# Attention scores of two units in ten full steps instead of sixteen of four widths, in a post-norm transformer block on one core

## The chip, the cores and the metric

The kernel runs on one core of a Trainium2 chip. The metric is the device time of one execution in microseconds (us); lower is better. TensorE is called PE here, VectorE DVE, ScalarE ACT, GpSimd POOL, and SyncE SP, as in the profile.

## The reference

The input x is 8 batches of 512 tokens of 256 features. Everything is float32. The block computes attention with a memory term, a layer norm, a mixture of eight experts, and a second layer norm. Cut to what matters:

```python
qkv = (x @ qkv_w.T + qkv_b).reshape(B, T, 3, H, dh)          # B 8, T 512, H 16 heads, dh 16
scores = einsum('bhtd,bhsd->bhts', q, k) * dh ** -0.5
scores = where(causal, -inf, scores)
seq_out = einsum('bhts,bhsd->bhtd', softmax(scores), v)
# four more projections of x give "write" and "read" lines of each head; decayed sums over the
# tokens of their outer products, read by the read lines, give one gate per token:
gated = mean over heads of sigmoid(mem_score * mem_scale) * sigmoid(x @ memg_w.T + memg_b)
x = layernorm(x + (seq_out + gated * (x @ memv_w.T + memv_b)) @ out_w.T + out_b)
# experts: softmax over ten gates, the two largest, eight true experts of 256 x 256
combine_w = weights of the two chosen experts, normed over the true ones
x = layernorm(x + einsum('te,teh->th', combine_w, einsum('td,edh->teh', x, expert_w) + expert_b))
```

## The kernel before

**Units.** The attention of a batch is done in four units of four heads (`UNITS`, 32 in all). `project_qk` makes, for two units at a time, q and k with the four heads of a unit on four strips of 32 partitions. A score product thus has a contraction of 32 rows, and products of different strips can stand beside each other on TensorE.

**Two kinds of products.** Softmax needs the largest score of each query. So each score is computed twice. The first time, `mx` (L194), has queries on the partitions and keys along the columns; DVE reduces it to the negated row maximum (`negmax`, `negdia`). `turn_largest` transposes the maxima of a unit and a DMA (`qk<-nt`) puts them into a spare row of q. The second time, `sc` (L198), has keys on the partitions and queries along the columns, with the maximum already subtracted by that spare row; ACT takes the exponential into `pe` (L226), POOL clears what is not causal on the diagonal block (L228), and `values` (L250) multiplies `pe` with v into one bank `po`, which also gets the sums for the division.

**Causal widths.** With four tiles of 128 tokens, query tile t has 128 (t + 1) keys that count, and key tile j has 512 - 128 j queries. So there are products of 128, 256, 384 and 512 columns.

**Steps.** One call of `products(u, i, pr)` is a step: the maxima of unit u + 1 for one query tile and two heads, on two strips, and beside them the scores of unit u (or u - 1) for one key tile of the same width and two heads, on the other two strips. A unit has eight steps, two for each width. `mx` and `sc` have one buffer each of two banks, one bank for each head (`psA`, bufs=1).

**The mask of the maxima.** For the first 12 units (`BYPASS`), and for a unit's last step later, a product of a bfloat16 mask with the identity (L207, 128 columns) adds -1e30 to the diagonal block, and DVE reduces the whole at once (L208). Otherwise ACT copies the diagonal block out (`dia`, L212), POOL masks the copy (L213), DVE reduces the rest of the row (L216), and one step later the copy (L219).

**What fills the time between steps.** Everything else is written as generators: the lines and the memory sums (`lines`, `memory_sums`, `finish`), the preparation of a batch (`prepare`), its attention output and first norm (`front`: `pa`, `px`, `pg`), and its experts (`all_experts`: `pex` L772 with two DVE operations L776 each, `pbias`). After each step, `fill` adds a credit, the step's share in `TAKE` less what is fixed there (projections `PQ`, `PV`, values `PO`), plus `MORE` (or `EARLY` before the first batch is ready), and lets the generators go on until their stated costs have used it up. What of the share finds no work is filled with idle products (`warm`, L843). A generator that yields `STEP`, `POOL`, `LESS` or `CALM` goes on only at a later turn, or only when POOL has not been given too much in this one. The order on each engine is then exactly the order in which the program was written (`in_this_order`).

**Buffers.** `psB` has three banks for all other products; `pe` has four buffers; `po` one bank. SP's queue issues nearly all DMAs.

Of the kernel before, what the change touches and what calls it, by code (L numbers as in the profile page):

```python
# [20 lines left out]
NG = 4  # L21
# [5 lines left out]
TAKE = (0.85, 1.6, 1.35, 1.1)  # L27
EARLY, MORE = 0.6, 0.9
WARM = 0.3
PV, PQ, PO = 1.2, 2.15, (1.05, 0.85, 0.65, 0.45)  # L30
ROUNDS = (2, 1, 1, 1)
# [14 lines left out]
for _n, _w in (("ob", D), ("gb", NE), ("mgb", H), ("msc", H), ("dec", H), ("mix", 1)):  # L46
    ROW[_n] = (_at, _at + _w)
    _at += _w
# [29 lines left out]
def block_kernel(ctx, tc, x, xT, wqk, bqk, wtok, wod, memv, memvb, row, gw, we, eb, out):  # L78
# [26 lines left out]
    nc.gpsimd.dma_start(rows, row.to_broadcast([P, NROW]))  # L105
# [17 lines left out]
    for b in range(1, B):  # L123
# [10 lines left out]
    mask_ts = const.tile([P, P], BF16, name="mask_ts")  # L134
    nc.gpsimd.memset(mask_ts, 0.0)
    nc.gpsimd.affine_select(out=mask_ts, in_=mask_ts, compare_op=ALU.is_ge, fill=MASKED,
                            base=0, pattern=[[-1, P]], channel_multiplier=1)
# [16 lines left out]
    ob2 = const.tile([P, D], F32, name="ob2")  # L154
# [3 lines left out]
    UNITS = [(b, g) for b in range(B) for g in range(NG)]  # L158
    qk = {}
# [24 lines left out]
    def products(u, i, pr):  # L184
        m, t = u + 1, (0, 3, 2, 1)[i]
        v, j = (u, i - 1) if i else (u - 1, NT - 1)
        n = T - j * P
        mx = m < len(UNITS) and psA.tile([P, 2, T], F32, tag="mx", name=f"mx{m}_{t}_{pr}")
        sc = 0 <= v < len(UNITS) and psA.tile([P, 2, T], F32, tag="sc", name=f"sc{v}_{j}_{1 - pr}")
        for h in range(2):  # L190
            if mx:

                r = slice(32 * (2 * pr + h), 32 * (2 * pr + h) + 32)
                nc.tensor.matmul(mx[:, h, :n], qk[m, 0][r, n - P : n], qk[m, 1][r, :n], start=True, stop=m >= BYPASS and (i, pr) != LAST)  # L194
            if sc:

                r = slice(32 * (2 - 2 * pr + h), 32 * (2 - 2 * pr + h) + 32)
                nc.tensor.matmul(sc[:, h, :n], qk[v, 1][r, j * P : (j + 1) * P], qk[v, 0][r, j * P :], start=True, stop=True)  # L198
        behind = list(diagonal)
        diagonal.clear()  # L200
        if mx:
            if m not in negmax:
                negmax[m] = [att.tile([P, 4, NT], F32, name=f"{n_}{m}", tag=n_) for n_ in ("negmax", "negdia")]
            most, least = (v[:, 2 * pr : 2 * pr + 2, t] for v in negmax[m])
            if m < BYPASS or (i, pr) == LAST:
                for h in range(2):
                    nc.tensor.matmul(mx[:, h, n - P : n], identb, mask_ts, start=False, stop=True)  # L207
                nc.vector.tensor_reduce(least, mx[:, :, :n], AX.X, ALU.max, negate=True)  # L208
            else:

                dia = ffp[0].tile([P, 2, P], F32, tag="dia", name=f"dia{m}_{t}_{pr}")
                nc.scalar.copy(dia, mx[:, :, n - P : n])  # L212
                nc.gpsimd.affine_select(out=dia, in_=dia, compare_op=ALU.is_ge, fill=MASKED,  # L213
                                        base=0, pattern=[[0, 2], [-1, P]], channel_multiplier=1)
                if t:
                    nc.vector.tensor_reduce(most, mx[:, :, : n - P], AX.X, ALU.max, negate=True)  # L216
                diagonal.append((least, dia))
        for to, dia in behind:
            nc.vector.tensor_reduce(to, dia, AX.X, ALU.max, negate=True)  # L219
        if mx and m >= BYPASS and (i, pr) == LAST:  # L220
            most, least = negmax[m]
            for hs, ts in ((slice(0, 2), slice(1, NT)), (slice(2, 4), slice(2, NT))):
                nc.vector.tensor_tensor(least[:, hs, ts], least[:, hs, ts], most[:, hs, ts], ALU.min)
        if sc:
            pe = att.tile([P, 2, T], F32, tag="pe", name=f"pe{v}_{j}_{1 - pr}", bufs=4)
            nc.scalar.activation(pe[:, :, :n], sc[:, :, :n], AF.Exp, scale=DH**-0.5)  # L226

            nc.gpsimd.affine_select(out=pe[:, :, :P], in_=pe[:, :, :P], compare_op=ALU.is_ge, fill=0.0,  # L228
                                    base=0, pattern=[[0, 2], [1, P]], channel_multiplier=-1)
            pes[j, 1 - pr] = pe  # L230

    def turn_largest(u):

        pt = bank(f"pt{u}")
        nc.tensor.transpose(pt[:H, :P], negmax.pop(u)[1].rearrange("p j i -> p (j i)"), ident)
# [4 lines left out]
    negmax, diagonal = {}, []  # L240
    LAST = NT - 1, 1
    pes, pos = {}, {}

    def values(u, j):

        b, g = UNITS[u]
        if j == 0:
            pos[u] = psO.tile([P, T], F32, tag="po", name=f"po{u}")
        for h in range(4):
            nc.tensor.matmul(pos[u][32 * h : 32 * h + 32, j * P :], v_aug[b % 2][:, j, 4 * (g // 2) + h, g % 2 : g % 2 + 2].rearrange("p q d -> p (q d)"),  # L250
                             pes.pop((j, h // 2))[:, h % 2, : T - j * P] if h % 2 else pes[j, h // 2][:, 0, : T - j * P],
                             start=(j == 0), stop=(j == NT - 1))
        if j == NT - 1:
# [10 lines left out]
    def invert(b, part):  # L264

        s = st[b]
        if part == 0:
            s["rec"] = att.tile([P, T // 8], F32, name=f"rec{b}", tag="rec")
            nc.sync.dma_start(s["rec"], s["den"].rearrange("k j q (e t) -> (k j q e) t", e=8))
# [18 lines left out]
    def fold_values():  # L288
# [9 lines left out]
        for n in range(2):  # L298
# [7 lines left out]
            else:  # L306
                nc.vector.tensor_tensor(ob2, pw[:, :D], vec("ob"), ALU.add)
# [161 lines left out]
    def memory_sums(half):  # L469
# [35 lines left out]
        for n, (h, c) in enumerate(todo):  # L505
# [24 lines left out]
            if rounds[1] >= ROUNDS[(turn[0] - 1) // 2 % NT]:  # L530
# [6 lines left out]
    def finish(half, h0, rm):  # L537
# [8 lines left out]
        for n, to, by in ((1, sm, of_heads), (2, sm2, rm)):  # L546
            for c in range(0, NT, 2):
                cs = slice(c, c + 2)
                yield LESS
                q = memp.tile([P, 2, 8 * HALF, 6], F32, tag="q", name=f"q{n}{half}_{h0}_{c}", bufs=2)  # L550
# [274 lines left out]
    def advance(it):  # L825
# [5 lines left out]
        elif asks == CALM and (at == turn[0] or turn[0] % (2 * NT) == 0):  # L831
            return None
        elif asks == STEP and at == turn[0] or asks == POOL and turn[1] or asks == LESS and turn[1] > 1:
# [11 lines left out]
    def fill(need, most=3.0, least=0.0):  # L845
# [5 lines left out]
    def filled():  # L851
        turn[:] = turn[0] + 1, 0
        for it in list(chains):
            for _ in range(2):
# [33 lines left out]
    U = len(UNITS)  # L888
    for u in range(-1, U + 1):
        b, g = UNITS[u] if 0 <= u < U else (0 if u < 0 else B, -1)  # L890
        for i in range(NT if u < U else 2):
            for pr in range(2):
                need = TAKE[i]
                if (i, pr) == (0, 0) and 0 <= u < BYPASS:
                    turn_largest(u)
                    need -= 0.3
                products(u, i, pr)
                if pr == 0:
                    if i == 0 and BYPASS <= u < U:
                        turn_largest(u)  # L900
                        need -= 0.3
                    if u % 2 == 0 and u + 2 < U and i in (1, 2):
                        project_qk(u + 2, i - 1)
                        need -= PQ
                    if g == NG - 1 and b + 1 < B:
# [81 lines left out]
```

## Time and profile before

| | us |
|---|---|
| median of 3 runs (lowest, highest) | 933.14 (932.42, 936.82) |
| span of the profiled execution, first to last instruction | 931.2 |
| PE busy, matmuls (5280) | 863.4 |
| PE busy with weight loads (overlap the matmuls) | 415.6 |
| DVE busy (1460) | 625.8 |
| ACT busy (754) | 346.5 |
| POOL busy (726) | 383.9 |
| first and last score group | 11.3 and 805.3 |

The profile gives no other time for its execution than the span; the median of the runs is 1.9 us above it, and that is taken for what lies around the first and the last instruction. A row of the costliest groups names the line, the engine, the operation, out<-in by the program's names, the shapes and the count, then the busy time and the mean of one in ns, then the idle time of the engine just before, with what ended it. PE's records overlap each other, since matmuls are pipelined and their ends are modelled; what a group costs is therefore read from its start to the start of what follows.

### The profile page before, as it was taken

Reading aid. Unit: us, or ns where it says so; the run is one execution under the profiler, and the core shown is the slowest. Engines: PE = TensorE matmul, PEld = TensorE weight load, DVE = VectorE, ACT = ScalarE, POOL = GpSimd, SP = SyncE. Lnnn points to the kernel's source line nnn. Section 1 sums busy time; section 2 is a strip of 40 time slices with the busy share of each in tenths; the row PEclk is TensorE's granted clock in tenths of the full one; section 3 lists DMA queues with packets and bytes.
Section 4 is the critical chain, followed back from the end, with each engine's and each line's share of the span. In section 5 each row is a group of like instructions: output and inputs, shape, how many; then the busy total and the mean of one; then the engine's idle time right before and its main releaser. Section 6 shows DMA issues by size and latency. Waiting matters only on the chain.

```text
span 931.2 us, 14645 instructions
## 1 busy us (share of the span) xinstructions
PE 863.4 (93%) x5280; PEld 415.6 (45%) x5280; DVE 625.8 (67%) x1460; ACT 346.5 (37%) x754; POOL 383.9 (41%) x726
## 2 busy tenths in 40 slices
PE   8999978788899889999999999999999999989997
PEld 5545444444355444453435344534353335344443
DVE  2344678986876787768685667666666675577765
ACT  4355624344334434435444444353434332100000
POOL 1168684526483855424353245324532352110000
PEclk9999989999999999999999999999999999989999
DMA  7300000000010101000200010001100010010000
GB/s 256 102 13 14 8 7 5 2 2 2 29 46 2 48 5 46 2 1 5 70 1 2 3 48 24 2 5 35 36 2 3 26 47 1 3 47 0 23 28 17
DMA packets 25512, 23.73 MB, mean 25 GB/s; under 512 B 8348, under 2 KB 21180, under 8 KB 25440
## 3 DMA queue, kind: packets, MB, share of 16 engines
q1 hardware_dynamic: 24336, 22.24, 7.5%
q8 instruction: 41, 0.67, 0.3%
q10 hardware_dynamic: 1056, 0.40, 0.2%
q0 software_dynamic: 48, 0.16, 0.2%
q14 instruction: 31, 0.25, 0.1%
HBM read 16.75 MB, written 4.73 MB: 23 GB/s over the span
## 4 chain that ended last, share of the span: by engine, by line
PE 63%; DVE 20%; POOL 6%; issue 4%; ACT 4%; DMA 3%; ACTq 0%; POOLq 0%; SPq 0%; DVEq 0%
PE pex L772 22%; PE mx L194 13%; PE po L250 6%; PE pq L167 4%; PE pa L653 3%; PE pa L656 3%; DVE negdia L208 3%; DVE x L776 3%; PE sc L198 2%; DVE negmax L216 2%; DMA s<-w 2%; PE pv L177 2%; DVE ou L520 2%; DVE pr L522 2%; DVE rm L502 1%
## 5 line engine op out<-in xcount | busy, mean ns | idle before, releaser
L194 PE MATMUL mx<-qk,qk 32*128 32x128 f32 (+3 forms) x1024 | 221.4, 486 | 35.9 <-DVE negdia L208 23.9
L772 PE MATMUL pex<-ws,x1T 128*128 128x512 f32 x512 | 243.7, 613 | 5.5 <-DVE x L776 4.9
L226 ACT ACTIVATE pe<-sc 128x1024 f32<-128x1024 f32 (+3 forms) x256 | 181.5, 709 | 144.6 <-PE sc L198 137.2
L198 PE MATMUL sc<-qk,qk 32*128 32x512 f32 (+3 forms) x1024 | 211.2, 485 | 3.0 <-DMA qk<-nt 1.8
L776 DVE SCALAR_TENSOR_TENSOR x<-pex,cw,x 128x256 f32<-128x256 f32 x256 | 123.2, 481 | 90.6 <-PE pex L772 85.3
L228 POOL TENSOR_SCALAR_AFFINE_SELECT pe<-pe 128x256 f32<-128x256 f32 x256 | 105.7, 413 | 176.1 <-ACT pe L226 170.2
L194 PEld LDWEIGHTS mx<-qk,qk 32*128 32x128 f32 x1024 | 85.4, 184 | 147.6 <-DVE negdia L208 41.4
L772 PEld LDWEIGHTS pex<-ws,x1T 128*128 128x128 f32 x512 | 92.0, 192 | 118.4 <-issue 101.2
L208 DVE TENSOR_REDUCE negdia<-mx 128x2 f32<-128x512 f32 (+3 forms) x116 | 92.3, 795 | 68.1 <-PE mx L207 67.4
L213 POOL TENSOR_SCALAR_AFFINE_SELECT dia<-dia 128x256 f32<-128x256 f32 x140 | 57.3, 409 | 178.7 <-ACT dia L212 178.5
L212 ACT COPY dia<-mx 128x256 f32<-128x256 f32 x140 | 52.1, 372 | 209.5 <-PE sc L198 203.9
L216 DVE TENSOR_REDUCE negmax<-mx 128x2 f32<-128x768 f32 (+2 forms) x100 | 74.0, 740 | 47.4 <-ACT dia L212 46.6
L250 PE MATMUL po<-pe,v_aug 128*32 128x512 f32 (+3 forms) x1024 | 96.7, 450 | 0.4 <-POOL pe L228 0.4
L198 PEld LDWEIGHTS sc<-qk,qk 32*128 32x128 f32 x1024 | 79.3, 184 | 11.9 <-issue 4.5
L167 PE MATMUL pq<-xt,wq 128*128 128x512 f32 x128 | 64.7, 630 | 3.3 <-DVE x L787 2.7
L219 DVE TENSOR_REDUCE negdia<-dia 128x2 f32<-128x256 f32 x140 | 57.4, 410 | 7.9 <-POOL dia L213 7.9
L171 ACT ACTIVATE qk<-pq,bq 128x512 f32<-128x512 f32 x64 | 46.2, 774 | 27.5 <-PE pq L167 27.5
L512 PE MATMUL pm<-ou,dm 128*128 128x144 f32 x256 | 46.6, 312 | 2.4 <-DVE pr L522 2.3
L631 POOL TENSOR_TENSOR rr_b<-rs_b,half 128x4 f32<-128x4 f32 (+1 forms) x11 | 9.2, 840 | 95.8 <-DVE rs_b L629 95.7
L512 PEld LDWEIGHTS pm<-ou,dm 128*128 128x128 f32 x256 | 36.9, 198 | 18.3 <-issue 13.5
L483 POOL TENSOR_TENSOR ou<-jw,jf 128x288 f32<-128x288 f32 x64 | 44.3, 698 | 1.3
L843 PE MATMUL idle<-ident 128*128 128x128 f32 x192 | 35.3, 313 | 2.9 <-POOL ident masks.py:199 2.8
(175 smaller groups left out, 1031.5 us busy)
## 6 DMA issues: line engine op xcount, KB each, us to landing
xt<-in_xT SPq DMA_DIRECT2D x8, 512.0 KB
x<-in_x SPq DMA_DIRECT2D x8, 512.0 KB
recs<-dr SPq DMA_DIRECT2D x16, 256.0 KB
out_y<-x SPq DMA_DIRECT2D x32, 128.0 KB
ws<-in_we SPq DMA_DIRECT2D x2, 1024.0 KB
s<-w SPq DMA_DIRECT2D x8, 127.0 KB
qk<-nt ACTq DMA_DIRECT2D x32, 8.0 KB
wq<-in_wqk SPq DMA_DIRECT2D x3, 128.0 KB
```

The source lines that it names most:

```text
L167: nc.tensor.matmul(pq, wq[:, k, w, g // 2, :], xt[:, b, k, :], start=(k == 0), stop=(k == KC - 1))
L194: nc.tensor.matmul(mx[:, h, :n], qk[m, 0][r, n - P : n], qk[m, 1][r, :n], start=True, stop=m >= BYPASS and (i, pr) != LAST)
L198: nc.tensor.matmul(sc[:, h, :n], qk[v, 1][r, j * P : (j + 1) * P], qk[v, 0][r, j * P :], start=True, stop=True)
L208: nc.vector.tensor_reduce(least, mx[:, :, :n], AX.X, ALU.max, negate=True)
L216: nc.vector.tensor_reduce(most, mx[:, :, : n - P], AX.X, ALU.max, negate=True)
L219: nc.vector.tensor_reduce(to, dia, AX.X, ALU.max, negate=True)
L226: nc.scalar.activation(pe[:, :, :n], sc[:, :, :n], AF.Exp, scale=DH**-0.5)
L228: nc.gpsimd.affine_select(out=pe[:, :, :P], in_=pe[:, :, :P], compare_op=ALU.is_ge, fill=0.0, base=0, pattern=[[0, 2], [1, P]], channel_mu ...
L250: nc.tensor.matmul(pos[u][32 * h : 32 * h + 32, j * P :], v_aug[b % 2][:, j, 4 * (g // 2) + h, g % 2 : g % 2 + 2].rearrange("p q d -> p (q ...
L512: nc.tensor.matmul(pm[:, i * HALF * 36 : (i + 1) * HALF * 36], dms[h + i], ou[:, i], start=True, stop=True)
L772: nc.tensor.matmul(pe, x1T[:, k, c * P : (c + 1) * P], ws[:, k, 2 * ep : 2 * ep + 2, :].rearrange("p e h -> p (e h)"), start=(k == 0), sto ...
L776: nc.vector.scalar_tensor_tensor(x1[:, c, :], pe[:, e * D : (e + 1) * D], cw[:, c, 2 * ep + e : 2 * ep + e + 1], x1[:, c, :], ALU.mult, AL ...
```

## The change

The scores of two units (a pair) are cut into ten steps that each fill the two banks of `mx` and of `sc`, 512 columns for each head. A step holds one piece of 512, or two pieces of 128 and 384, or two of 256 that belong to the two units of the pair. `mx` runs seven steps ahead of `sc` (`LAG`). A mask product now covers the whole bank (512 columns, L227 of the kernel after) and comes first in its step, with `start=True`; the row products add to it. The masks are needed in all ten steps of the first six pairs and in two steps (`LASTS`) of the others. The value products of earlier steps stand between the masks and the row products, one or two key tiles at a time, so that five steps of ten have them. The diagonal copies of a step with two pieces hold 512 columns in place of 256. The exponential always covers 1024 columns. The shares of `fill` are set anew: `TAKE` 1.9 for every step, `MORE` 1.5 and `EARLY` 1.0, at most two memory products a step, POOL's limits a step raised. To make room, three small tiles are smaller: the bias of the output is loaded straight into `ob2` by its own DMA, `rec` has one buffer, and `q` in `finish` holds one query tile in place of two.

The diff, cut to its core:

```diff
-TAKE = (0.85, 1.6, 1.35, 1.1)
-EARLY, MORE = 0.6, 0.9
+TAKE = 1.9
+EARLY, MORE = 1.0, 1.5
-ROUNDS = (2, 1, 1, 1)
+ROUNDS = 2
...
-    nc.gpsimd.dma_start(rows, row.to_broadcast([P, NROW]))
+    nc.gpsimd.dma_start(rows, row[:, D:].to_broadcast([P, NROW]))
+    ob2 = const.tile([P, D], F32, name="ob2")
+    nc.gpsimd.dma_start(ob2, row[:, :D].to_broadcast([P, D]))
...
-    mask_ts = const.tile([P, P], BF16, name="mask_ts")
+    masks = const.tile([P, 5, P], BF16, name="masks")
...
+    SPAN, LAG, LASTS, VALUES = 10, 7, (5, 9), (9, 11, 13, 15)
+    STINTS = len(UNITS) // 2 * SPAN
...
-    def products(u, i, pr):
-        m, t = u + 1, (0, 3, 2, 1)[i]
-        v, j = (u, i - 1) if i else (u - 1, NT - 1)
-        n = T - j * P
+    def pieces(k):
+        p, pos = divmod(k, SPAN)
+        u = 2 * p + (pos > 5)
+        return p, pos, (((u, 3, 0),), ((u, 0, 0), (u, 2, P)), ((u, 1, 0), (u + 1, 1, 2 * P)))[(pos % 6) // 2]
...
+    def products(k, kv, shown):
...
+            masked = 2 * p < BYPASS or pos in LASTS
...
         for h in range(2):
-            if mx:
-                r = slice(32 * (2 * pr + h), 32 * (2 * pr + h) + 32)
-                nc.tensor.matmul(mx[:, h, :n], qk[m, 0][r, n - P : n], qk[m, 1][r, :n], start=True, ...)
-            if sc:
-                r = slice(32 * (2 - 2 * pr + h), 32 * (2 - 2 * pr + h) + 32)
-                nc.tensor.matmul(sc[:, h, :n], qk[v, 1][r, j * P : (j + 1) * P], qk[v, 0][r, j * P :], start=True, stop=True)
+            if mx and masked:
+                nc.tensor.matmul(mx[:, h], identb, mask_of(pos % 6 // 2), start=True, stop=False)
+        for u, js in shown:
+            values(u, *js)
+        for x in range(2):
+            for h in range(2):
+                if x < len(mxs):
+                    m, t, c, n = mxs[x]
+                    r = slice(32 * (2 * pr + h), 32 * (2 * pr + h) + 32)
+                    nc.tensor.matmul(mx[:, h, c : c + n], qk[m, 0][r, n - P : n], qk[m, 1][r, :n], start=not masked, ...)
+                if x < len(scs):
+                    v, j, c, n = scs[x]
+                    r = slice(32 * (2 * prv + h), 32 * (2 * prv + h) + 32)
+                    nc.tensor.matmul(sc[:, h, c : c + n], qk[v, 1][r, j * P : (j + 1) * P], qk[v, 0][r, j * P :], start=True, stop=True)
...
-            nc.scalar.activation(pe[:, :, :n], sc[:, :, :n], AF.Exp, scale=DH**-0.5)
+            nc.scalar.activation(pe, sc, AF.Exp, scale=DH**-0.5)
...
-            s["rec"] = att.tile([P, T // 8], F32, name=f"rec{b}", tag="rec")
+            s["rec"] = att.tile([P, T // 8], F32, name=f"rec{b}", tag="rec", bufs=1)
...
-        elif asks == CALM and (at == turn[0] or turn[0] % (2 * NT) == 0):
+        elif asks == CALM and (at == turn[0] or (turn[0] - 1) % SPAN in LASTS):
...
-        elif asks == STEP and at == turn[0] or asks == POOL and turn[1] or asks == LESS and turn[1] > 1:
+        elif asks == STEP and at == turn[0] or asks == POOL and turn[1] > 1 or asks == LESS and turn[1] > 2:
...
+    shown = {2: (0, (0,)), 4: (0, (1, 3)), 6: (0, (2,)), 8: (1, (0, 2))}
+    for k in range(STINTS + LAG + 2):
+        kv = k - LAG
+        need = TAKE
...
+        if at == 0 and 0 < kv <= STINTS:
+            vals.append((2 * p - 1, (1, 3)))
+        products(k, kv, vals)
+        need -= sum(PO[j] for _, js in vals for j in js)
...
+        fill(need, least=need)
+        if k < STINTS and k % SPAN in LASTS:
+            turn_largest(2 * (k // SPAN) + LASTS.index(k % SPAN))
```

In place of the row products' own order of before (products, mask, projections, values, fill), the order of a step on PE is now: masks, values, row products, projections, fill.

## The prediction

> **What bounds the kernel now.** I read the page first (busy shares, costliest groups), then the stretches, TensorE's waits, and last its timeline, which alone gives what a group of products costs from its start to the start of what follows.
>
> From the page:
>
> ```profile
> PE 863.4 (93%) x5280; PEld 415.6 (45%) x5280; DVE 625.8 (67%) x1460; ACT 346.5 (37%) x754; POOL 383.9 (41%) x726
> ...
> L194 PE MATMUL mx<-qk,qk 32*128 32x128 f32 (+3 forms) x1024 | 221.4, 486 | 35.9 <-DVE negdia L208 23.9
> ...
> L843 PE MATMUL idle<-ident 128*128 128x128 f32 x192 | 35.3, 313 | 2.9 <-POOL ident masks.py:199 2.8
> ```
>
> PE is the bound, and its idle time (68 us) is mostly one wait, 35.9 us ahead of the row maxima's products. Stretches (PE busy is the first number after the length):
>
> ```profile
> 100.00:400.00 300.00, 261.69 (x1927) 138.81 (x1927) 229.41 (x481) 123.60 (x249) 169.71 (x302) 0.96 0.05 16
> 400.00:800.00 400.00, 390.23 (x2430) 171.92 (x2429) 270.14 (x670) 167.62 (x346) 154.76 (x324) 1.00 0.06 18
> ```
>
> PE idles 38.3 us of the first 300 and 9.8 us of the next 400. Its waits, total, times, longest:
>
> ```profile
> PE mx L194 <- DVE negdia L208: 23.9, 25, 2.9
> PE mx L194 <- DVE negmax L216: 9.5, 16, 3.6
> ```
>
> There is one mx buffer, so a step's products wait until VectorE has reduced the last step's. The timeline of PE:
>
> ```profile
> 29.88 0.28 PE L207 MATMUL mx<-mask_ts,identb 128*128 128x128 bf16 x2
> 30.00 0.68 PE L351 MATMUL pl<-wt,xt 128*128 128x272 f32 x2
> ...
> 500.13 0.69 PE L194 MATMUL mx<-qk,qk 32*128 32x512 f32 x1
> ...
> 500.15 0.69 PE L198 MATMUL sc<-qk,qk 32*128 32x512 f32 x1
> 500.67 0.59 PE L194 MATMUL mx<-qk,qk 32*128 32x512 f32 x1
> ...
> 501.20 1.13 PE L177 MATMUL pv<-wt,xt 128*128 128x256 f32 x4
> ...
> 504.18 1.98 PE L772 MATMUL pex<-ws,x1T 128*128 128x512 f32 x4
> 506.10 0.58 PE L194 MATMUL mx<-qk,qk 32*128 32x384 f32 x1
> ...
> 744.27 0.48 PE L194 MATMUL mx<-qk,qk 32*128 32x256 f32 x1 [0.30 <-DVE negmax L216]
> ...
> 744.92 0.94 PE L843 MATMUL idle<-ident 128*128 128x128 f32 x6
> ...
> 746.67 0.28 PE L207 MATMUL mx<-mask_ts,identb 128*128 128x128 bf16 x2
> 746.89 0.85 PE L250 MATMUL po<-pe,v_aug 128*32 128x384 f32 x8
> ...
> 750.96 0.37 PE L194 MATMUL mx<-qk,qk 32*128 32x128 f32 x1
> ...
> 751.40 0.28 PE L235 MATMUL pt<-ident,negdia 128*16 128x128 f32 x1
> ...
> 788.38 3.70 PE L772 MATMUL pex<-ws,x1T 128*128 128x512 f32 x8
> 792.01 0.59 PE L198 MATMUL sc<-qk,qk 32*128 32x384 f32 x2
> ```
>
> A float32 product is two records. The four products of a step (two mx, two sc, each on its own 32 rows) start within 0.02 us: they run side by side. Start to next start, a step takes 0.44 us at 128 columns (750.96 to 751.40), 0.65 at 256, 1.07 at 512: 0.21 per 128 columns and 0.22 whatever the width. That fixed part is what packing can save.
>
> **The change, part by part.** The multiplications stay: both programs have 512 mx, 512 sc and 512 value products of the same widths. The columns of two units stay too: 4 x (128+256+384+512) = 10 x 512.
>
> 1. Groups: 8 + 256 + 2 = 266 steps with products before, 160 + 7 = 167 after: 99 fewer at 0.22 = -21.8 us.
> 2. Way in: four pex records ahead of a group take 1.92 (504.18 to 506.10), eight take 3.63, so a record is 0.43 and the change to 32 rows 0.21. Some of it is paid between other full-array work too: four pv records took 1.06 ahead of a group (512.64 to 513.70) and 0.97 ahead of idle products (501.20 to 502.17), a difference of 0.09. Between 0.09 and 0.21 I take 0.14: -13.9 us (bounds -8.9, -20.8).
> 3. Values: 128 groups of one key tile become 80, five for two units. A group took 0.35 at 128 columns (503.83 to 504.18) and 1.00 at 512 (509.15 to 510.15), so 0.14 is fixed: 48 x 0.14 = -6.7 us. The move ahead of the row products costs nothing by itself: full, column, row, full is as many changes as full, row, column, full.
> 4. Masks: before, 116 pairs of 128 columns, 62 of them ahead of values at 0.22 (746.67 to 746.89) and the rest at 0.12 (29.88 to 30.00): 20.1 us. After, 80 pairs of 512 columns (60 steps of the first six pairs, two of each of the other ten). No bfloat16 product that wide is in the trace. One of 128 took 0.06, a float32 record of 512 0.43; a bfloat16 128 streams about half as long as a float32 record's 0.107, so 512 should take 0.06 + 3 x 0.053 = 0.22, a pair 0.44 and 0.10 for leaving the full array: 80 x 0.54 = 43.2, or +23.1 us. Bounds: width free, 80 x 0.22, -2.5; as a float32 record, 80 x 0.96, +57. I take the bfloat16 row as the nearest.
> 5. Idle products: 96 become 119, 46 more records at 0.134 ((0.94 - 0.27) / 5 at 744.92): +6.2 us, or 0 where they fill a wait.
> 6. Order inside a group. Nine of ten steps hold two widths on a row group, and the sc pieces are other widths than the mx pieces beside them (128 then 384 beside 512, say). No group in the trace mixes widths. If each row group runs its own pieces one behind the other, a step takes 1.07: 0 us. If no second piece starts before all first pieces end, the ten steps last 7168 columns in place of 5120: 16 x 0.21 x 16 pairs = +54 us. The row for the near end: at 500.15 the fourth product's first record starts, and only at 500.67 the first product's second record; so a later product doesn't queue behind an earlier one on other rows. I take 0 and keep 54 for the range.
> The Trainium skill speaks against this. "TensorE: Matmul & The Clock Gate", Part 3, "The mechanism", holds that matmuls start and end strictly in program order, whatever rows they use. Read strictly, a piece would also wait for the slower pieces ahead of it, and the sum would move towards the 54 us; the rows at 500.15 and 500.67 agree with it only if the order is that of records and not of products. By the rows the sum is the 910 below, by the strict rule an estimate of up to 964.
> 7. The wait on VectorE. From a group's end (503.82) the diagonal's copy ran 503.95 to 504.32, the reduction of 768 from 504.35 to 505.31: 1.5 us that other PE work has to cover. Steps were 2.98 us apart (266 from 11.3 to 805.3), 0.83 of it in the group itself (221.4 / 266): 2.1 us of cover, less in many. After, the planner grants 1.9 + 1.5 = 3.4 us a step less the values. So part of the 35.9 us goes. Not all: it lies in the stretch of 100 to 400, where VectorE is 76% busy, and of its work only some 11 us goes: for each of ten unmasked pairs of units 15.3 us of reductions (14 x 0.41 + 4 x 0.95 + 6 x 0.69 + 2 x 0.42 + 0.8 of minima) become 14.3 (5 x 0.41 + 5 x 0.95 + 8 x 0.69 + 1.2 + 0.8), and little for the masked ones. I take a third: -12 us (bounds 0, -36).
> 8. What is late next: a values group now reads the pe tile of the step just ahead. Group end to end of select was 503.82 to 505.72, 1.9 us; with a copy of 512 (0.59 for 0.37) and a select of twice the blocks (0.82 for 0.41) 2.5 us. All five such steps follow steps with the full 3.4 us of cover: 0. Behind a stalled values group the row products and all PE work would stand; bound +40 us (80 x 0.5).
> 9. The tail: 124 expert products stand behind the last group in place of 104, and 32 of the front's in place of 16: 20 x 0.86 + 16 x 0.43 = 24 us moved. From 800 on PE is busy 118.8 of 132 us, 90%, so a tenth of it is lost: +2.4 us.
> Taken at nothing: ScalarE's 256 exponentials become 160 of 1.03 us (181.5 to 165) and 140 copies 80, GpSimd's selects become fewer and longer, both engines at about 40%; uncovered, they would add 0.2 to 0.4 us a step, which point 8 holds. The second bias DMA and one more mask select on GpSimd's queue at the start (some 1 us) end before the first group at 11.3, which waits for projections; else +1. One buffer for the inverse sums puts SP's load of them behind a store of a batch earlier.
>
> Sum: -21.8 - 13.9 - 6.7 + 23.1 + 6.2 + 0 - 12 + 0 + 2.4 = -22.7 on the profiled span of 931.2: 908.5. The median of the runs is 933.14, 1.9 above that span; with it **910 us**.
>
> **Rivals.**
> - Slower, by point 6: pieces side by side wait for the widest. 910 + 54 = 964. For it: no mixed group was seen. Against: the start times at 500.15. It decides from 23 us on, 0.15 us in each of the 150 mixed steps.
> - Half of that, 26 us: 936, no change that can be told.
> - Slower, by point 8: the pe chain is longer than its cover in the early steps, where idle products fill only 1.9 us: 910 + 40 = 950.
> - VectorE binds the stretch of 100 to 400 whatever PE does: nothing of the 12 us, 922. For it: 76% busy there.
> - All of the wait goes: 910 - 24 = 886. For it: 400 to 800 already idles only 2%.
> - That the packing isn't there is out: the built program has the groups as counted.
>
> **How the numbers follow.** The forecast, 896 to 918 by points 2, 4 and 7, has 0.38; 922 has 0.14; 886 has 0.12; 936 has 0.10; 964 has 0.17; 950 has 0.09. A measurement of this kernel can tell about 0.5% (4.7 us) from no change: faster 0.38 + 0.14 + 0.12 = 0.64, same 0.10, slower 0.26. The range, 884 to 952, leaves out most of the 964 case and a little below 886; the faster cases alone hold 884 to 924.
>
> **What would show it.** A mixed step of about 1.07 to 1.1 us from first product to next start (over 1.25: point 6 is wrong); mask pairs of about 0.5; idle ahead of mx (or of the masks) near 24 us; hardly any idle ahead of po. A PE with more idle, or DVE over 80% from 100 to 400, would mean that the gain was lost to VectorE; values that wait for GpSimd's select would make the forecast wrong.

## The result, and the profile after

The kernel after takes 950.48 us in the median of its runs (946.83 to 952.10), beside 934.01 for the kernel before: a ratio of 1.016, with an interval of 1.0121 to 1.020. It is 1.6% slower; 910 was forecast. The profiled execution has a span of 945.1 us and took 946.83 as a whole, so 13.9 us were lost on the span where the sum had -22.7.

The page after first: busy time by engine, then three of the costliest groups.

```profile
PE 848.6 (90%) x5254; PEld 453.6 (48%) x5254; DVE 616.8 (65%) x1394; ACT 328.3 (35%) x598; POOL 366.5 (39%) x652
...
L236 PE MATMUL mx<-qk,qk 32*128 32x128 f32 (+3 forms) x1024 | 187.4, 470 | 5.4 <-DVE negmax L287 5.4
...
L328 PE MATMUL po<-pe,v_aug 128*32 128x512 f32 (+3 forms) x1024 | 98.4, 461 | 7.8 <-POOL pe L304 7.8
...
L227 PE MATMUL mx<-masks,identb 128*128 128x512 bf16 x160 | 48.1, 382 | 16.9 <-DVE negdia L287 14.2
```

PE is busy for 14.8 us less than before, and yet it ends later: it idles 96.5 us (945.1 - 848.6) where it idled 67.8. No other engine has more to do. (TensorE's weight loads, which overlap its products, are busy 38.0 us more; but so they are, with 35.1 us, in the faster kernel with the values behind, below.) The lost time is waiting.

The groups with different shapes kept apart show where it stands. The first row is the weight loads of the values, the second the transposes of the maxima, ahead of which PE idled 3.2 us before.

```profile
L328 PEld LDWEIGHTS po<-pe,v_aug 128*32 128x32 f32 x1024 | 28.7, 112 | 73.5 <-issue 43.7 <-POOL pe L304 21.9 <-POOL gb L688 1.5
...
L312 PE MATMUL pt<-ident,negdia 128*16 128x128 f32 x32 | 8.7, 272 | 28.2 <-DVE negdia L294 16.0 <-DVE negdia L287 9.3 <-DVE lg L776 2.4
```

The stretches of 100 to 400 and 400 to 800 (PE busy is the first number after the length):

```profile
100.00:400.00 300.00, 252.45 (x1891) 145.62 (x1891) 217.32 (x426) 126.56 (x229) 174.61 (x302) 0.95 0.05 14
400.00:800.00 400.00, 373.51 (x2403) 189.67 (x2405) 258.13 (x607) 152.41 (x240) 141.22 (x262) 0.99 0.06 20
```

PE's idle time rises from 38.3 to 47.6 us in the first and from 9.8 to 26.5 in the second, while VectorE's share falls in both. So it isn't VectorE's load that binds. Waits of PE (total, times, longest):

```profile
PE pt L312 <- DVE negdia L294: 16.0, 13, 2.2
PE mx L227 <- DVE negdia L287: 14.2, 16, 2.1
PE pt L312 <- DVE negdia L287: 9.3, 10, 1.9
...
PE po L328 <- POOL pe L304: 7.8, 5, 4.1
PE mx L236 <- DVE negmax L287: 5.4, 9, 1.3
...
PE mx L227 <- DVE negmax L287: 2.0, 3, 1.2
```

The waits at mx fell from 33.4 us to 21.6 (14.2 + 5.4 + 2.0). In their place stand two that the sum didn't have: the transposes' 25.3 (16.0 + 9.3) and the values'.

The timeline of PE, a step of mixed pieces:

```profile
490.41 0.37 PE L236 MATMUL mx<-qk,qk 32*128 32x128 f32 x1
490.42 0.69 PE L241 MATMUL sc<-qk,qk 32*128 32x512 f32 x1
...
490.95 0.60 PE L241 MATMUL sc<-qk,qk 32*128 32x512 f32 x2
491.06 0.49 PE L236 MATMUL mx<-qk,qk 32*128 32x384 f32 x2
491.49 0.70 PE L851 MATMUL pex<-ws,x1T 128*128 128x512 f32 x1
```

Pieces of 128 and 384 beside a piece of 512 take 1.08 us from first start to next start, as a plain step of 512 does. And the last step of a unit, with its masks, its values, and the transposes behind it:

```profile
498.01 0.59 PE L227 MATMUL mx<-masks,identb 128*128 128x512 bf16 x2
498.54 1.50 PE L328 MATMUL po<-pe,v_aug 128*32 128x512 f32 x16
499.96 0.48 PE L236 MATMUL mx<-qk,qk 32*128 32x256 f32 x1
...
503.31 0.28 PE L312 MATMUL pt<-ident,negdia 128*16 128x128 f32 x1 [2.19 <-DVE negdia L294]
```

The mask pair takes 0.53 us. Then 1.4 us of values run, and only then the row products, whose bank VectorE must reduce before the transpose. PE stands still for 2.19 us.

Start to next start, summed over the whole program (a wait behind a group or inside its records is counted with the group; "values behind" and "best" are experiments below):

| us | before | after | values behind | best |
|---|---|---|---|---|
| row products (mx and sc) | 221.7 | 197.3 | 187.9 | 193.9 |
| masks | 22.3 | 42.5 | 42.6 | 21.1 |
| values | 88.9 | 101.1 | 97.0 | 91.6 |
| idle products | 43.2 | 45.2 | 37.2 | 42.0 |
| memory sums `pm` | 65.5 | 68.1 | 60.9 | 66.0 |
| span | 931.2 | 945.1 | 907.4 | 890.2 |

The values show a wait that the matmul's row hides. Undisturbed, the five groups of a pair take 0.996, 1.001 twice, 0.570 and 1.428 us (medians): 79.9 for 16 pairs, 6.6 less than the 86.5 that 128 groups of before take at their medians. Measured were 101.1, so 21.2 us are waiting, though the matmul's row names 7.8. The 31 groups of key tiles 1 and 3 ahead of row products have a median of 1.00 and a mean of 1.48. The weight loads' row above names 21.9; what the matmul's row doesn't name stands inside its stretched records.

### The profile page after: what moved, and what is told of

The parts are those of the page before. It is cut to its first block, busy times and chain, and to the rows that moved or that the text cites. A ratio compares the mean times of both kernels' runs of the same rounds, so it can differ in the third digit from the quotient of the medians.

```text
span 945.1 us, 14226 instructions
## 1 busy us (share of the span) xinstructions
PE 848.6 (90%) x5254; PEld 453.6 (48%) x5254; DVE 616.8 (65%) x1394; ACT 328.3 (35%) x598; POOL 366.5 (39%) x652
## 4 chain that ended last, share of the span: by engine, by line
PE 69%; DVE 18%; issue 4%; POOL 4%; ACT 3%; POOLq 0%; DVEq 0%; ACTq 0%
PE pex L851 21%; PE mx L236 10%; PE po L328 8%; PE sc L241 6%; PE pq L178 6%; DVE negdia L287 4%; PE mx L227 3%; PE pv L188 3%; PE idle L922 3%; PE pa L732 3%; PE pa L735 2%; PE pl L429 2%; DVE x L855 2%; DVE ou L598 2%; DVE pr L600 2%
## 5 line engine op out<-in xcount | busy, mean ns | idle before, releaser
L297 ACT ACTIVATE pe<-sc 128x1024 f32<-128x1024 f32 x160 | 164.3, 1027 | 172.2 <-PE sc L241 162.9
L304 POOL TENSOR_SCALAR_AFFINE_SELECT pe<-pe 128x256 f32<-128x256 f32 (+1 forms) x224 | 97.6, 449 | 264.3 <-ACT pe L297 256.9
L236 PE MATMUL mx<-qk,qk 32*128 32x128 f32 (+3 forms) x1024 | 187.4, 470 | 5.4 <-DVE negmax L287 5.4
L241 PE MATMUL sc<-qk,qk 32*128 32x384 f32 (+3 forms) x1024 | 186.5, 470 | 0.9 <-ACT pe L297 0.8
L287 DVE TENSOR_REDUCE negdia<-mx 128x2 f32<-128x768 f32 (+3 forms) x114 | 100.0, 902 | 124.3 <-PE sc L241 93.3
L279 POOL TENSOR_SCALAR_AFFINE_SELECT dia<-dia 128x256 f32<-128x256 f32 (+1 forms) x80 | 41.6, 520 | 143.1 <-ACT dia L277 141.8
L241 PEld LDWEIGHTS sc<-qk,qk 32*128 32x128 f32 x1024 | 88.8, 188 | 15.0 <-ACT pe L297 2.0
L277 ACT COPY dia<-mx 128x256 f32<-128x256 f32 (+1 forms) x80 | 38.3, 479 | 116.0 <-PE sc L241 79.9
L328 PEld LDWEIGHTS po<-pe,v_aug 128*32 128x32 f32 x1024 | 28.7, 112 | 73.5 <-issue 43.7
L227 PE MATMUL mx<-masks,identb 128*128 128x512 bf16 x160 | 48.1, 382 | 16.9 <-DVE negdia L287 14.2
L182 ACT ACTIVATE qk<-pq,bq 128x512 f32<-128x512 f32 x64 | 46.2, 773 | 18.2 <-PE pq L178 17.6
```

The lines of the kernel that those rows point to most:

```text
L182: nc.scalar.activation(t, pq, AF.Identity, bias=bq[:, n : n + 1], scale=bq[:, 2 * NG + odd : 2 * NG + odd + 1])
L227: nc.tensor.matmul(mx[:, h], identb, mask_of(pos % 6 // 2), start=True, stop=False)
L236: nc.tensor.matmul(mx[:, h, c : c + n], qk[m, 0][r, n - P : n], qk[m, 1][r, :n], start=not masked, stop=not masked or x == len(mxs) - 1)
L241: nc.tensor.matmul(sc[:, h, c : c + n], qk[v, 1][r, j * P : (j + 1) * P], qk[v, 0][r, j * P :], start=True, stop=True)
L287: nc.vector.tensor_reduce(out_of(i, w), part, AX.X, ALU.max, negate=True)
L297: nc.scalar.activation(pe, sc, AF.Exp, scale=DH**-0.5)
```

## The experiments

The theory: the packing costs and saves what the sum said, and the **place of the values** loses it, in two ways. As the last thing ahead of the row products they wait for GpSimd's select of the step just ahead, with all of PE behind them. And they stand before the row products instead of behind them, so they no longer cover VectorE's reductions ahead of the transposes. Rivals: the transposes were put too early; VectorE is the bound whatever the order; a DMA of the maxima comes late; the credit of `fill` is too small. Ratios are to the kernel before on the same chip.

| experiment | median, us | ratio (95%) | profiled span |
|---|---|---|---|
| after | 950.48 | 1.016 (1.0121 to 1.020) | 945.1 |
| transposes one step later | 942.67 | 1.0104 (1.007 to 1.0139) | 938.8 |
| values behind the row products | 908.54 | 0.9735 (0.971 to 0.976) | 907.4 |
| both | 927.40 | 0.9939 (0.9909 to 0.9968) | 928.0 |
| before, transposes early | 939.37 | 1.0065 (1.0037 to 1.0094) | 935.2 |
| before, values ahead | 951.16 | 1.0188 (1.0157 to 1.0218) | 951.4 |
| values behind in the transposes' steps alone | 926.63 | 0.9905 (0.9871 to 0.9938) | 925.2 |
| values behind in the other steps alone | 931.59 | 0.9977 (0.9949 to 1.0005) | 927.3 |
| values a step older | 930.70 | 0.9966 (0.9941 to 0.9991) | 926.3 |
| values behind, narrow masks | 900.28 | 0.9641 (0.9597 to 0.9685) | 898.4 |
| the same, `MORE` 2.0 (best) | 891.72 | 0.9547 (0.951 to 0.9584) | 890.2 |
| the same, `MORE` 1.1 | 896.61 | 0.9596 (0.956 to 0.9632) | 894.9 |
| after, `MORE` 2.1 | 948.16 | 1.0143 (1.0098 to 1.0189) | 948.4 |

### Values behind the row products

```diff
-        for u, js in shown:
-            values(u, *js)
         for x in range(2):
...
                     nc.tensor.matmul(sc[:, h, c : c + n], ...)
+        for u, js in shown:
+            values(u, *js)
```

The copy of a finished `po` moves behind the step's products with them.

> Edit: the value products stand after the row products of the same step, as before the change, instead of directly ahead of them; only their place moves. Theory W: the select has one group (1.07 us) more time, the values' wait (about 27 us, most of it inside the records of the values) falls under 8, time 925 to 938. Rival V: the same wait turns up at the next row products, since exponentials are later; time 945 to 955.

The span falls by 37.7 us, to 23.8 below that of before. The time lies far below the expected 925 to 938, and yet the values' wait, which was to fall under 8 us, is still 17.1 in their sum (97.0 - 79.9): the expectation counted the select alone, and not what the values cover in their old place. PE's idle time is 68.2 us (907.4 - 839.2), as before the change. Its largest waits on the attention's tiles:

```profile
PE mx L227 <- DVE negdia L287: 12.1, 7, 2.1
...
PE pt L312 <- DVE negdia L294: 7.4, 6, 1.7
PE po L328 <- POOL pe L304: 4.8, 2, 3.1
PE mx L234 <- DVE negmax L287: 4.7, 4, 1.8
```

The same step of the timeline as the one shown above:

```profile
474.90 0.59 PE L227 MATMUL mx<-masks,identb 128*128 128x512 bf16 x2
475.42 0.48 PE L234 MATMUL mx<-qk,qk 32*128 32x256 f32 x1
...
476.50 1.50 PE L328 MATMUL po<-pe,v_aug 128*32 128x512 f32 x16
478.77 0.28 PE L312 MATMUL pt<-ident,negdia 128*16 128x128 f32 x1 [0.77 <-DVE negdia L294]
```

The 1.4 us of values now stand between the row products and the transposes. The wait is 0.77 where it was 2.19, 1.42 less, and the step ends 3.87 us after its masks started where it took 5.30. The one move carries the whole loss; the next two runs part it. The clock that TensorE was granted, as a share of full speed, doesn't explain it: the profile's mean over the span is 0.981 before, 0.977 in the kernel after and 0.980 here. What is missing to 1, times the span, is 17.7, 21.7 and 18.1 us, so by this estimate the clock holds at most 4.0 of the 13.9 us that the change lost and 3.6 of the 37.7 that the move gives.

### The same move in some steps only

Two kernels put the values behind the row products by position, the first in the two steps of a pair that transposes follow, the second in the three others.

```diff
+        late = kv % SPAN in (2, 8)
-        for u, js in shown:
+        for u, js in () if late else shown:
             values(u, *js)
...
+        for u, js in shown if late else ():
+            values(u, *js)
```

> Edit on the changed kernel: values stand behind the row products in two of the five value steps of a pair only, those in which a unit's maxima end and the transposes follow; in the other three they stay ahead. Theory W: the wait of the transposes falls from 33 us to about 13 and a part of the values' wait goes: 918 to 932. Rival S (it is the values' wait for the select alone, spread over all five): two fifths of 42 us at most and no change at pt: 930 to 936. Rival V: 943 to 952.

The second has `(4, 6, 0)` in place of `(2, 8)`.

> The other half: values stand behind the row products in the three value steps that no transposes follow. Theory W: the values' wait (27 us) falls to about 10, the wait of the transposes stays near 30 us: 922 to 934. Rival S: 923 to 928 with the transposes' wait lower too. Rival V: 943 to 952.

The view of one tile says until what its engine sat idle (us, times; a matmul's wait and its weight load's are both in it). The transposes' tile pt in the kernel after:

```profile
  DVE negdia L294: 27.1, 19
  DVE negdia L287: 12.8, 13
```

The same tile with the values behind in the transposes' steps alone, where the two lines are L298 and L291:

```profile
  DVE negdia L298: 15.1, 12
...
  DVE negdia L291: 4.4, 2
```

And with the values behind in the other steps alone:

```profile
  DVE negdia L298: 27.1, 19
  DVE negdia L291: 13.1, 13
```

The values' tile po in the kernel after:

```profile
  POOL pe L304: 29.7, 35
```

With the values behind in the transposes' steps alone, the select being L308:

```profile
  POOL pe L308: 28.3, 33
```

In the other steps alone:

```profile
  POOL pe L308: 16.7, 20
```

Both medians lie in the ranges of the main theory; the rival of the select alone needed pt unchanged in the first kernel and shorter in the second. Each kernel lessens one wait (39.9 us to 19.5 at pt, 29.7 to 16.7 at po) and leaves the other about where it was. Their spans fall by 19.9 and 17.8 us, 37.7 together, which is what the whole move gave. In the medians of all runs the ratios fall by 0.0255 and 0.0183, 0.0438 together for the 0.0425 of the whole move; each of these differences is good to some 0.005, so the exact sum of the spans is partly luck, and the first part may be the larger. The loss thus has two parts of similar size, and they add within the noise: cover taken from the transposes, and row products held behind values that wait for the select.

### Values a step older, still ahead of the row products

```diff
-    shown = {2: (0, (0,)), 4: (0, (1, 3)), 6: (0, (2,)), 8: (1, (0, 2))}
+    shown = {3: (0, (0,)), 5: (0, (1, 3)), 7: (0, (2,)), 8: (1, (0, 2))}
```

The group at position 0 moves to 1 as well, so four of the five groups read an exponential that is a step older.

> Edit on the changed kernel: values stay ahead of the row products, but four of the five groups of a pair come one step later, so that their exponentials and selects are a whole step older. Theory W: no wait for the select is left, and three of ten value steps move out of the way of the transposes: 912 to 930. Rival P (what costs is that the row products stand behind 0.6 to 1.4 us of values, not the wait for the select): the time stays at 938 to 952 though nothing waits for the select.

The view of the tile po: the values' wait falls to about a third, and PE's own row of waits for the select is gone.

```profile
  POOL pe L304: 10.8, 19
```

The span falls by 18.8 us, close to what the other steps alone gave; the median, 930.70, is just above the range of the main theory and far below the rival's. The transposes still wait 21.1 us on PE's row, for 25.3: the group that was at position 2 no longer stands ahead of them. The granted clock is 0.988 in this profile, so only 11.1 us are missing by it where the kernel after misses 21.7; by this estimate up to 10.6 of the 18.8 us may be the clock's, and the size of the select's part is less sure than that the wait went. The wait is thus a matter of how soon the values ask, not of GpSimd's load, which is the same (365.0 us busy for 366.5).

### Transposes one step later, with the values where the change puts them and behind

```diff
         products(k, kv, vals)
+        if 0 < k <= STINTS and (k - 1) % SPAN in LASTS:
+            turn_largest(2 * ((k - 1) // SPAN) + LASTS.index((k - 1) % SPAN))
...
-        if k < STINTS and k % SPAN in LASTS:
-            turn_largest(2 * (k // SPAN) + LASTS.index(k % SPAN))
```

> Edit: the transposes of a unit's maxima stand after the next step's row products instead of at the end of the unit's last step. Theory W (the gain went into two new waits of TensorE: transposes that wait for VectorE's last maxima, some 26 us, and values that wait for GpSimd's select, some 27 us): idle ahead of pt falls from 28 us to under 6, idle ahead of the values and masks stays, time 922 to 935. Rival V (VectorE is simply late, whoever waits for it): what pt no longer waits, the masks and row products do; idle ahead of them rises by 15 us or more, time 943 to 952. Rival D (the DMA of the maxima has no time left): sc waits for it, time above 950.

The transposes' wait on PE's rows goes from 25.3 us to 0.3, and only 6.3 us of span come back (the ratio falls by 0.0056). The waits at mx take up much of the rest, 34.3 us for 21.6; their three largest rows among PE's waits:

```profile
PE mx L227 <- DVE negdia L287: 21.3, 24, 2.1
...
PE mx L236 <- DVE negdia L287: 7.4, 7, 1.3
...
PE mx L236 <- DVE negmax L287: 3.8, 7, 1.1
```

With the values ahead, the next step's mx needs the same reduction a little later. The transposes were only the first to meet it. Moving the one that waits, and giving it no cover, moves the wait. The time is just below the range of the rival that saw the wait move on, and above that of the theory that saw it vanish.

With the values behind the row products as well (the second diff added to the first experiment's):

> Both edits of the two runs beside it. Theory W: the gains add, 25 + 20 us: 900 to 915. Rival V: within 10 us of the changed kernel, 940 to 955.

This missed: 927.40 us, 19 more than with the values moved alone. A wait that hardly stood there with the values moved alone (0.5 us by tile) appears, 23.0 by tile and 11.7 among PE's waits:

```profile
PE sc L239 <- DMA qk<-nt: 11.7, 13, 2.3
```

The transposed maxima go by DMA into the spare row of q that sc reads, in both kernels in the very next step. In the kernel with the transposes alone moved, where that wait is 1.6 us by tile, a group of values of key tiles 1 and 3 (1.00 us undisturbed) stands between, ahead of that step's row products: from the transposes to these products it is 2.97 us for the first unit of a pair and 4.07 for the second (medians). With the values behind, it is 2.03 and 2.69. In one such step the DMA is issued just as the row products start, and sc begins 1.84 us later:

```profile
488.24 0.53 ACTq L315 DMA_DIRECT2D qk<-nt  x1
...
488.24 1.12 PE L234 MATMUL mx<-qk,qk 32*128 32x512 f32 x2
...
490.08 0.66 PE L239 MATMUL sc<-qk,qk 32*128 32x512 f32 x1 [0.71 <-DMA qk<-nt]
```

So here the values' move took away the DMA's cover, as the change's own move took the transposes'. (The clock, 0.971 for 0.980, can hold up to 8.8 of the 20.6 us of span by the estimate used above.) The change's early transposes have a use, and the place to put cover is ahead of them.

### The kernel before, with each of the two moves

The transposes at the end of the unit's last step, as the change has them:

```diff
-                if (i, pr) == (0, 0) and 0 <= u < BYPASS:
-                    turn_largest(u)
+                if (i, pr) == (0, 0) and 0 <= u < U:
                     need -= 0.3
...
                 fill(need, least=need)
+                if (i, pr) == (NT - 1, 1) and u + 1 < U:
+                    turn_largest(u + 1)
```

> The kernel before, with the transposes of a unit's maxima moved to the end of the unit's last step, after its filling work, as the changed kernel has them; all else as before. Theory W: each of 31 transposes now waits for VectorE's last reductions, idle ahead of pt rises from 3 us to 12 to 25, time 942 to 958. Rival V: the row products of the next step would have waited for VectorE anyway; time 931 to 938.

It costs 0.65%: 939.37 us, between the two ranges and far less than the main theory expected. PE's waits at pt for the maxima rise only from 2.9 to 5.2 us (1.8 more end with another instruction of VectorE). In this order the values still stand behind the row products, and the fill too, so the transposes are covered. Their early place alone isn't the loss. Then the values directly ahead of the row products:

```diff
+                if pr == 1:
+                    v, j = (u, i - 2) if i > 1 else (u - 1, NT - 2 + i)
+                    if v >= 0:
+                        values(v, j)
+                        need -= PO[j]
                 products(u, i, pr)
...
-                    v, j = (u, i - 2) if i > 1 else (u - 1, NT - 2 + i)
-                    if v >= 0:
-                        values(v, j)
-                        need -= PO[j]
```

> The kernel before with one part of the change: value products directly ahead of the row products of their step instead of behind them. Its values read exponentials that are two steps old, so there is no wait for the select to expect; what moves is that the row products, and with them the reductions, start 0.36 to 1.0 us later in every second step, and that the values no longer cover VectorE's time behind them. Theory P (place costs by itself, through lost cover): idle ahead of the next products grows by 10 to 25 us, 942 to 960. Theory S (only the young exponentials cost): 930 to 938.

1.9% slower, without any packing, as the theory of the place expected: about what the whole change lost. PE's waits at mx rise from 33.4 to 43.9 us, and those at pt from 2.9 to 8.7, of which 7.2 are in the third row:

```profile
PE mx L194 <- DVE negdia L208: 28.4, 34, 1.9
PE mx L194 <- DVE negmax L216: 15.5, 18, 3.2
...
PE pt L235 <- DVE negdia L208: 7.2, 8, 2.2
```

The values of this kernel are two steps old, and I had expected no wait for the select there. It rose all the same, by tile from 5.4 us to 19.1. So that part of the expectation was wrong, and how much of the 18 us is select and how much lost cover wasn't parted here.

### Narrow masks

The row products start the bank, and masks of 128 columns on the diagonal blocks alone follow them; values behind both.

```diff
-        for h in range(2):
-            if mx and masked:
-                nc.tensor.matmul(mx[:, h], identb, mask_of(pos % 6 // 2), start=True, stop=False)
...
+        if mx and masked:
+            for x, (m, t, c, n) in enumerate(mxs):
+                for h in range(2):
+                    nc.tensor.matmul(mx[:, h, c + n - P : c + n], identb, masks[:, 2], start=False, stop=x == len(mxs) - 1)
```

> Edit on top of e2_values_after: the mask products go back to 128 columns and behind the row products (272 of 128 columns in place of 160 of 512). Theory W: mask products fall from 42 us to about 25 with their mode changes, and TensorE waits at the row products for what it waited at the masks: 888 to 900. Rival V: VectorE's reductions start later by the masks' time, and the waits of TensorE for VectorE grow by what is saved: 904 to 914.

The masks' time falls by 21.4 us (42.6 to 21.2), the span by 9.0, to just above the range that the main theory gave. The row products' sum rises by 6.1 and that of the memory sums by 5.4: part of the wide masks' time lay where PE would have waited anyway.

### The credit

`MORE` 2.0 and 1.1 in place of 1.5 in the kernel with narrow masks, then 2.1 in the kernel after.

```diff
-EARLY, MORE = 1.0, 1.5
+EARLY, MORE = 1.0, 2.0
```

> Edit on top of e4_narrow_masks: MORE 2.0 in place of 1.5, so each step after the first batches gets 0.5 us more filling work (158 expert products before the last score group in place of 132). Theory W: TensorE's remaining waits for VectorE (some 40 us ahead of row products, 14 ahead of transposes) shrink by the better cover, 890 to 898. Rival U (those waits lie in the memory stage, before any expert work, where VectorE is the bound): within 4 us of 900.

> Edit on top of e4_narrow_masks: MORE 1.1 in place of 1.5 (110 expert products before the last score group). Theory W: less cover, the waits of the transposes and row products grow, 904 to 918. Rival U: within 4 us of 900.

> The changed kernel with MORE 2.1 in place of 1.5, values still directly ahead of the row products (160 expert products before the last score group). Theory W: more filling work covers part of the waits of transposes and values, 928 to 942, but not what the place of the values costs. Rival C (the place of the values does no harm, the change only has too small a credit): 905 to 918. Rival U: 945 to 952.

In the kernel after, more credit does next to nothing (948.16): the transposes still wait 18.2 us and the values 9.4 on PE's rows, so too little filling work was not the cause. In the kernel with narrow masks, 2.0 gives 891.72, the best of all, 4.5% below the kernel before and within the main theory's range. The waits that were to shrink hardly did, though: at mx 20.0 us to 19.6, at pt 10.4 to 7.8. Its stretches:

```profile
100.00:400.00 300.00, 265.14 (x2101) 162.56 (x2103) 234.82 (x469) 134.43 (x239) 182.05 (x316) 0.95 0.05 16
400.00:800.00 400.00, 389.35 (x2438) 199.02 (x2436) 280.33 (x683) 142.61 (x230) 139.26 (x252) 1.00 0.07 21
```

From 400 to 800 PE idles 10.7 us, about as in the kernel before. VectorE does more in each stretch than in the kernel after: 78% of the first 300 us, where that one has 72%. VectorE could thus do more than it was given. But with 1.1 the ratio is 0.9596 where 1.5 had 0.9641, in intervals that overlap: no slower, within the rival's 4 us of 900, where the main theory had 904 to 918. The credit also decides which filling work stands in which step, and the time doesn't follow it in one direction. Why stays open. The change also raised the most that the credit can hold, from 3.0 to 4.0 us, and let a generator go on three times in a turn in place of two; neither was run by itself.

## Why the prediction was wrong

By its own steps:

- **Point 3 failed**: "The move ahead of the row products costs nothing by itself". I counted the changes of the array's shape, and those are as many as before. I did not ask what the values stop covering, nor what stands behind them when they wait. With only this move undone the span is 907.4, where the sum had 908.5; put alone into the kernel before, it costs 18 us. Its other half, -6.7 for fewer groups, was right: 79.9 for 86.5 undisturbed.
- **Point 8 failed**: "All five such steps follow steps with the full 3.4 us of cover: 0". The values wait 21.2 us in their sum of start to next start, 24 more by tile than before. Credit is granted in stated costs and over steps, and it doesn't stand where it is needed: in the step at 503.51 the filling was 1.5 us of idle products. The rival at 950 had this mechanism and was given 0.09. It had the right time with half the reason.
- **A term was missing**: the transposes. The change moved them to the end of the unit's last step, where they read minima that VectorE makes from that very step. No point of the prediction names them. Their wait on PE's rows went from 2.9 to 25.3 us. This should have been costed by point 7's own chain: the copy and the reductions after a group take 1.5 us (at 503.31 the chain of two reductions and a minimum took 2.1, 501.16 to 503.25), and on the timeline of before the transposes at 751.40 stood behind the products of the step after, with a step's filling work between them and their producer.
- **Point 6 was right**, and the mechanism of the 964 rival is out. An undisturbed mixed step takes 1.07 to 1.08 us. Read strictly, the rule cited from the Trainium skill ("TensorE: Matmul & The Clock Gate", Part 3, "The mechanism") would have made a piece wait for slower pieces ahead of it; the step at 490.41, as long as a plain one of 512 columns, shows no such wait.
- **Point 4 was right**: 0.53 us a pair for the estimate of 0.54, 42.5 us in all for 43.2. The masks of before take 22.3, not the sum's 20.1, so the term was +20.2 for +23.1. But the narrow masks showed that not all of it lies on the path: 21.4 us less of masks gave 9.0.
- **Points 1 and 2**: the groups of before take 199 us at their medians, the 167 after 179 at the undisturbed 1.07: -20, for point 1's -21.8. The way in was not measured by itself, so point 2's -13.9 is neither shown nor refuted.
- **Point 5 had the count right and the size wrong**: 238 records for 192, but in 31 places instead of 47. Start to next start they take 45.2 us for 43.2, and 37.2 with the values behind: below nothing instead of +6.2.
- **Point 7**: -11.8 us at mx (33.4 to 21.6) for -12. It was no gain in the end, since the transposes met the same reduction first; when they were moved away, the wait at mx was back at 34.3. In the kernel with the values behind it is 19.3.
- **Point 9** stands: from the last row products on, PE has 22.5 us more to do (136.3 for 113.8), for the 24 that were to move, and idles 13.5 us of 149.8 where it idled 12.4 of 126.2: +1.1 for +2.4.

That the sum without the move comes within 1.1 us of its experiment is partly luck: there the values still wait 17.1 us (97.0 - 79.9) and the transposes 6.5 more than before, and the idle products (37.2 us, where the sum had 43.2 + 6.2) and the waits at mx (14.1 us less, where it had 12) give part of that back.

What is shown: the loss hangs on the values' place, in two parts that add within the noise. That the cover itself is the mechanism at the transposes is shown by the one step (1.42 us of values, 1.42 us less wait) and by the tile's waits. Open are the parts of the loss in the kernel before with the values moved, and the credit's effect.

## What to carry to other kernels

A move on an engine that works in order has two prices besides its own instructions: what the moved work may wait for, with everything behind it, and what it covered where it stood. Before costing a move at nothing, name the reader whose producer ran under it; for each short read-back (a transpose, a copy) placed right behind its producer, write down the producer's chain and the work that lies between. If a wait is found, put independent work ahead of the one that waits: moving the reader itself only hands the wait to the next reader, or to a DMA behind it.

## What the runs showed of the hardware

- Products of unequal widths on different row groups don't wait for one another: 128 and 384 beside 512 take 1.08 us (490.41 in the kernel after), and 2 x 256 beside 384 and 128 take 1.08 (475.42 with the values behind), as a plain step of 512 does (1.07).
- A group of values over two key tiles (128 and 384 columns) takes 1.00 us, as one tile of 512 does (0.996): the 0.14 us that a group costs at any width is paid once for both tiles.
- A wait can hide from the matmul's own row. The values' row names 7.8 us, their weight loads' row 21.9, and start to next start against the undisturbed time gives 21.2.
